# Input loads of later groups behind the weights, constant products in TensorE's planned pauses, and a last group that ends in two pairs

## The chip, the cores and the metric

The kernel runs on one core of one Trainium2 chip. The metric is the device time of one execution in microseconds (us). One core holds five engines with a queue each: TensorE (PE), VectorE (DVE), ScalarE (ACT), GpSimd (POOL) and SyncE (SP), which here issues nearly all transfers.

## The reference

There are 128 graphs of 128 nodes with 256 features each (`x`: 128 x 128 x 256) and an integer adjacency `adj` per graph. Four layers follow each other; each ends in a residual and a layer norm.

```python
A = (adj != 0)                               # layer 0: a gated graph network, 3 steps
for i in range(3):
    m = h @ weight[i]
    h = gru_cell(A^T @ m, h, w_ih, w_hh, b_ih, b_hh)
x = layernorm(x + h)
for W, a1, a2 in three attention layers:     # layers 1 to 3
    Wh = x @ W.T
    e = leaky_relu((Wh @ a1)[:, None] + (Wh @ a2)[None, :], 0.2)
    e = where(adj == 0, -huge, e)
    x = layernorm(x + softmax(e) @ Wh)
```

## The kernel before, in words

The 128 graphs are worked off in 32 groups of `G` = 4 graphs (512 columns). A group goes through `gru` (three steps of layer 0) and `gat` (layers 1 to 3), each with 128 partitions for the nodes or for one half of the features.

**Head.** Group 0 also prepares the weights. `hidden_weights` loads `w_hh` (two loads), scales it and builds the seven block sums of `whs` (`block_sums`, L432 to L436). `input_weights` multiplies each step's `gnn_wT` block with `w_ih` on TensorE (L466), evicts it with a scaling (L469, by `scale`, L411 or L413) and builds `wcs`. `transposed` (L555) turns the first two groups' x on TensorE; later groups are turned by transposing transfers (`turned`, L517). x is also split into three bf16 parts (L699), so that the sums over neighbours (L724) run in bf16.

**GRU.** A step multiplies both halves of the state and of the neighbour sums with the weights by a Strassen scheme (`strassen`, products at L650 into one of five PSUM tiles tagged `gate`). Between products into the same tile, ScalarE copies a partial sum out (L744, L748, L751) and VectorE adds (L655). The gates' arithmetic is at L762 to L801; the last step turns the state back on TensorE (L828) and adds it to x (L831); `layernorm` follows (L572 to L583).

**Attention.** A layer takes score sums on VectorE (L858, into a tile tagged `f` for one side), spreads one side over the columns (L870 and L877, or L887 for the last four groups), adds the mask and takes the maximum (L893), then Prelu (L897), Exp (L914), a transpose (L934 in the last four groups), the product with x (L964, four 128 x 128 products for each of two banks) and with W (L975, two products of 256 columns per graph), and the residual (L981). `deviation` squares on ScalarE with a sum (L591) and makes the variance (L595, L602); `power` raises it to -0.5 on GpSimd (L564). The scaling of layers 1 and 2 is folded into the next layer; the last one scales on ScalarE (L988) and stores the group (L990).

**Order.** No engine's order is written out by hand. Every operation is recorded with `plan.op(engines, fn, reads, writes, prio, ..., start)`: the engines that may run it with an assumed time in ns, its buffers, a priority and an earliest time. `Plan.order` plays the kernel through with these times (in four passes, with due times worked back from the pass before) and picks an engine, a slot of the buffer's pool and a place for each; it keeps the pass with the shortest end. Then the operations are emitted in that order, and each engine's queue holds its own in it. Times exist in the plan alone; on the chip an instruction waits only for its data, its buffers and its queue.

```python
plan.op({"SP": 450}, lambda e: nc.sync.dma_start(T(xs), x_g), writes=[xs], prio=prio)
...
order = plan.order()
with tc.manual_schedule():
    make_identity(nc, ident)
    nc.gpsimd.load_library(library_config.all_libraries[10])
    for o in order:
        o.fn(o.engine)
```

There are two slots each for x (`xs`) and the raw adjacency (`am`), three for `f`, five `gate` and three `bank` tiles in PSUM. The last four groups (`TAIL`) have a priority of their own and run their attention layers after the last GRU.

Of the kernel before, what the change touches and what calls it, by code (L numbers as in the profile page):

```python
# [12 lines left out]
AF = mybir.ActivationFunctionType  # L13
ALU = mybir.AluOpType
AX = mybir.AxisListType

P = 128
D = 256
KC = D // P
G = 4  # L20
# [6 lines left out]
EPS = 1e-5  # L27
# [281 lines left out]
def adj_resnorm_kernel(  # L309
# [14 lines left out]
    nc = tc.nc  # L324
    B = x.shape[0]
    NG = B // G
# [13 lines left out]
    tags = {t: (n, floats.get(t, 512)) for t, n in pools.items()}  # L340
    U16, BF16 = mybir.dt.uint16, mybir.dt.bfloat16
    BOTH = ("DVE", "POOL")
    LATER = (0.25, 1.75, -0.5, 0.25, 0.25, -1.0)
    plan = Plan({t: n for t, (n, _) in tags.items()}, own)
    slots = {t: [(psum if t in ("gate", "bank") else work).tile([P, w], F32, name=f"{t}{i}")
                 for i in range(n)] for t, (n, w) in tags.items() if w}

    def T(b):
        if b.at is None:
            width = 1  # L350
            for s in b.shape:
                width *= s
            at = slots[b.tag][b.slot][:, 0:width]
            if len(b.shape) == 2:
                at = at.rearrange("p (a b) -> p a b", b=b.shape[-1])
            elif len(b.shape) == 3:
                at = at.rearrange("p (a b c) -> p a b c", b=b.shape[-2], c=b.shape[-1])
            b.at = at
        return b.at
# [7 lines left out]
        return b  # L367

    for t in slots["f"]:
        nc.vector.memset(t, 0.0)  # L370

    nobody = [cycle([consts.tile([P, D], BF16, name=f"nobody{i}{j}") for j in range(2)]) for i in range(2)]
# [13 lines left out]
    neghalf = consts.tile([P, G], F32, name="neghalf")  # L388
# [20 lines left out]
    def scale(e, dst, src, by):  # L409
        if e == "ACT":  # L410
            nc.scalar.mul(dst, src, by)  # L411
        else:
            nc.vector.tensor_scalar(dst, src, by, None, op0=ALU.mult)  # L413
# [144 lines left out]
            res.append(dst)  # L558
        return res

    def power(ve, prio):

        rstd = Buf("v", G)
        plan.op({"POOL": 980}, lambda e: nc.gpsimd.tensor_tensor(T(rstd), T(ve), neghalf, ALU.pow),  # L564
                reads=[ve], writes=[rstd], prio=prio, port=BOTH, holds=False)
        return rstd

    def layernorm(y, dst, prio):
# [15 lines left out]
                T(dst)[:, b, :], T(y)[:, b, :], AF.Identity, bias=T(shift)[:, b:b + 1], scale=T(rstd)[:, b:b + 1]),  # L584
                reads=[(y, b), shift, rstd], writes=[(dst, b)], prio=prio)

    def deviation(y, before, prio):

        ss, ve = Buf("v", G), Buf("v", G)
        for b in range(G):  # L590
            plan.op({"ACT": 400}, lambda e, b=b: nc.scalar.activation(  # L591
                next(nobody[0]), T(y)[:, b, :], AF.Square, accum_out=T(ss)[:, b:b + 1]),
                reads=[(y, b)], writes=[(ss, b)], prio=prio, lag=85)
        if before is None:
            plan.op({"DVE": 78}, lambda e: nc.vector.tensor_scalar(  # L595
                T(ve), T(ss), 1.0 / D, EPS, op0=ALU.mult, op1=ALU.add),
                reads=[(ss, b) for b in range(G)], writes=[ve], prio=prio, port=BOTH)
        else:
            eps = Buf("v", G)
            plan.op({"DVE": 78}, lambda e: nc.vector.tensor_scalar(T(eps), T(before), EPS, None, op0=ALU.mult),  # L600
                    reads=[before], writes=[eps], prio=prio, port=BOTH)
            plan.op({"DVE": 78}, lambda e: nc.vector.scalar_tensor_tensor(  # L602
                T(ve), T(ss), 1.0 / D, T(eps), op0=ALU.mult, op1=ALU.add),
                reads=[(ss, b) for b in range(G)] + [eps], writes=[ve], prio=prio, port=BOTH)
        return ve

    def sums(ms, prio, banks=None, t=None):
# [24 lines left out]
    def strassen(gates, kept, prio):  # L632
# [40 lines left out]
        product(bx, N22, False)  # L673
        return o0, o1, bx

    def gru(g, stage):

        xs, ints = Buf("xs", G, D), Buf("am", G, P)
        prio = stage(g, 0)
        turn = Buf("gru")  # L680
        x_g = x[g * G:(g + 1) * G].rearrange("b n d -> n b d")
        plan.op({"SP": 450}, lambda e: nc.sync.dma_start(T(xs), x_g), writes=[xs], prio=prio)
        plan.op({"SP": 60}, lambda e: nc.sync.dma_start(T(ints).bitcast(I32), adj[g * G:(g + 1) * G].rearrange("b s t -> s b t")),
                writes=[ints], prio=prio)
        if g == 0:
            input_weights(0, (prio[0], -2))
            hidden_weights((prio[0], -2))
# [4 lines left out]
                reads=[ints], writes=[am, turn], prio=prio, port=BOTH)  # L692
# [20 lines left out]
        for i in range(STEPS):  # L713
            prio = stage(g, i)
# [129 lines left out]
    def gat(g, xc, far, stage):  # L844
# [5 lines left out]
        for l in range(3):  # L850
# [118 lines left out]
            for b0 in range(0, G, 2):  # L969
# [9 lines left out]
                for b in (b0, b0 + 1):  # L979
# [2 lines left out]
                                T(y)[:, b, :], T(b_)[:, (b - b0) * D:(b - b0 + 1) * D], T(rden)[:, b:b + 1],  # L982
                                T(xc)[:, b, :], op0=ALU.mult, op1=ALU.add),
                            reads=[b_, rden, (xc, b)], writes=[(y, b)], prio=prio)
            xc, ve = y, deviation(y, ve, prio)
            rstd = power(ve, prio)
        for b in range(G):
            plan.op({"ACT": 400}, lambda e, b=b: nc.scalar.mul(T(xc)[:, b, :], T(xc)[:, b, :], T(rstd)[:, b:b + 1]),  # L988
                    reads=[(xc, b), rstd], writes=[(xc, b)], prio=prio)
        plan.op({"SP": 60}, lambda e: nc.sync.dma_start(out[g * G:(g + 1) * G].rearrange("b n d -> n b d"), T(xc)),  # L990
                reads=[(xc, b) for b in range(G)], prio=prio)

    def stage(g, n):

# [4 lines left out]
        gat(g, *gru(g, stage), stage)  # L999

    order = plan.order()
    with tc.manual_schedule():
        make_identity(nc, ident)

        nc.gpsimd.load_library(library_config.all_libraries[10])
        for o in order:
            o.fn(o.engine)


# [40 lines left out]
```

## Time and profile before

| what | us |
|---|---|
| median of three runs (lowest, highest) | 2496.47 (2496.38, 2497.94) |
| the profiled execution: its own time | 2499.03 |
| its span, from the first to the last instruction | 2497.3 |
| TensorE, VectorE, ScalarE, GpSimd busy | 2459.4, 2192.5, 1950.0, 889.2 |
| gate products (L650) on the chain that ended last | 56% of the span |

The profile is of one execution. Its line numbers are those of the kernel before; in the changed kernel the same operations stand 2 to 21 lines further down up to the attention's end (L466 becomes L468, L555 L557, L564 L569, L591 L595, L650 L666, L724 L745, L744 L765, L828 L849, L887 L908, L934 L955, L964 L985, L975 L996, L981 L1002). A float32 product on TensorE appears as two records, so L964's eight products of a layer are x16. In a timeline a row gives start, length, engine, line, operation, tiles and count; in brackets stands how long the engine was idle before and what ended that.

### The profile page before, as it was taken

The page shows a single profiled execution, that of the slowest core. Times are in us where ns is not written, and L with a number is a line of the kernel's source. Part 1 is how long each engine was busy: PE and PEld are TensorE (multiplying, and loading weights), DVE is VectorE, ACT ScalarE, POOL GpSimd, SP SyncE. Part 2 cuts the span into 40 slices and gives each one's busy share as a digit, 9 for nine tenths or more (in the row PEclk, how much of TensorE's full clock was granted, in tenths as well). Part 3 has the DMA queues.
Part 4 walks back from the last instruction along what each step waited for, and adds up shares of the span by engine and source line. Part 5 has one row for each costly group of instructions (what it writes and reads, how often), then busy time and mean ns, then how long its engine had stood idle before and what let it go on. Part 6 is the DMA issues. An engine that isn't in the chain of part 4 may idle for free.

```text
span 2497.3 us, 42937 instructions
## 1 busy us (share of the span) xinstructions
PE 2459.4 (98%) x13716; PEld 2173.9 (87%) x13716; DVE 2192.5 (88%) x6443; ACT 1950.0 (78%) x4869; POOL 889.2 (36%) x1097
## 2 busy tenths in 40 slices
PE   8999999999999999999999999999999999999988
PEld 6888888888888888888888888888888888888877
DVE  6788899998998988989898989988989989877797
ACT  5667878888788887887977788887888877766578
POOL 3433335434334343345343344343343322212001
PEclk9999999999999999999999999999999999999989
DMA  5323323323423323333323333334333333010101
GB/s 140 64 42 65 81 65 76 73 57 75 82 64 77 72 54 75 81 65 76 75 54 77 81 64 72 61 72 77 76 69 69 73 63 68 22 39 18 39 1 35
DMA packets 456611, 161.41 MB, mean 65 GB/s; under 512 B 389184, under 2 KB 454720, under 8 KB 456384
## 3 DMA queue, kind: packets, MB, share of 16 engines
q1 hardware_dynamic: 455952, 158.65, 29.7%
q8 instruction: 108, 1.77, 0.3%
q14 instruction: 119, 0.97, 0.1%
q10 hardware_dynamic: 432, 0.01, 0.0%
HBM read 45.89 MB, written 16.78 MB: 25 GB/s over the span
## 4 chain that ended last, share of the span: by engine, by line
PE 77%; ACT 11%; DVE 8%; DMA 2%; issue 2%; POOL 0%; POOLq 0%; SPq 0%; ACTq 0%; DVEq 0%
PE gate L650 56%; PE bank L975 11%; PE bank L964 6%; PE bank L724 3%; ACT k L405 2%; ACT k L914 2%; DVE nobody L858 1%; DVE k L655 1%; ACT k L583 1%; ACT k L762 1%; DMA k<-k 1%; DVE k L981 1%; PE bank L728 1%; PE bank L466 1%; DMA xs<-in_x_dram 1%
## 5 line engine op out<-in xcount | busy, mean ns | idle before, releaser
L650 PE MATMUL gate<-k,whs 128*128 128x256 f32 x4032 | 1204.9, 380 | 9.7 <-ACT k L744 7.5
L650 PE MATMUL gate<-k,wcs 128*128 128x256 f32 x4032 | 1199.2, 379 | 0.0
L650 PEld LDWEIGHTS gate<-k,wcs 128*128 128x128 f32 x4032 | 766.0, 190 | 104.3 <-DVE k L407 0.2
L650 PEld LDWEIGHTS gate<-k,whs 128*128 128x128 f32 x4032 | 748.3, 190 | 120.9 <-issue 13.1
L655 DVE TENSOR_TENSOR k<-gate,k 128x512 f32<-128x512 f32 x576 | 391.6, 685 | 182.6 <-PE gate L650 121.3
L975 PE MATMUL bank<-gwT,k 128*128 128x256 f32 x1536 | 353.4, 382 | 0.6 <-DVE k L407 0.4
L564 POOL TENSOR_TENSOR v<-v,neghalf 128x4 f32<-128x4 f32 x128 | 154.2, 1204 | 526.3 <-DVE v L602 184.1
L858 DVE SCALAR_TENSOR_TENSOR nobody<-k,wa 128x256 bf16<-128x256 f32 x768 | 322.2, 463 | 4.4 <-ACT k L583 4.2
L975 PEld LDWEIGHTS bank<-gwT,k 128*128 128x128 f32 x1536 | 287.0, 190 | 38.8 <-DVE k L407 1.7
L762 ACT ACTIVATE k<-k,brz 128x512 f32<-128x512 f32 (+1 forms) x384 | 226.4, 620 | 76.8 <-DVE k L655 75.9
L405 ACT COPY k<-k 128x512 bf16<-128x512 bf16 (+1 forms) x308 | 223.5, 742 | 60.3 <-DVE k L801 42.9
L619 POOL TENSOR_TENSOR k<-k,k 128x256 f32<-128x256 f32 x257 | 207.2, 825 | 174.3 <-DVE k L801 127.7
L537 POOL TENSOR_TENSOR k<-k 128x512 f32<-128x512 f32 (+1 forms) x162 | 176.3, 1088 | 145.2 <-DVE k L801 66.2
L699 POOL TENSOR_TENSOR k<-xs 128x512 f32<-128x512 f32 x52 | 56.3, 1102 | 478.7 <-DMA xs<-in_x_dram 365.8
L591 ACT ACTIVATE nobody<-k 128x256 bf16<-128x256 f32 x384 | 156.2, 408 | 78.2 <-DVE k L981 78.1
L744 ACT COPY k<-gate 128x512 f32<-128x512 f32 x288 | 168.3, 585 | 61.9 <-PE gate L650 58.5
L877 POOL PARTITION_BROADCAST k<-k x336 | 154.1, 559 | 162.0 <-ACT k L405 85.9
L964 PEld LDWEIGHTS bank<-k,k 128*128 128x128 f32 x1536 | 187.3, 193 | 5.7 <-ACT k L405 0.8
L964 PE MATMUL bank<-k,k 128*128 128x128 f32 x1536 | 189.8, 277 | 0.9 <-ACT k L943 0.5
L511 ACT COPY k<-k 128x1024 uint16<-128x1024 uint16 x142 | 165.4, 1166 | 31.7 <-DMA k<-k 29.8
L405 ACT COPY k<-bank 128x512 f32<-128x512 f32 (+1 forms) x259 | 135.6, 530 | 64.2 <-PE bank L964 20.1
L897 ACT ACTIVATE k<-k,v 128x128 f32<-128x128 f32 x384 | 136.3, 399 | 59.9 <-DVE v L893 59.7
(117 smaller groups left out, 3580.5 us busy)
## 6 DMA issues: line engine op xcount, KB each, us to landing
xs<-in_x_dram SPq DMA_DIRECT2D x32, 512.0 KB, 4.0
k<-in_x_dram SPq DMA_DIRECT2D x32, 512.0 KB, 4.6
out_dram<-k SPq DMA_DIRECT2D x32, 512.0 KB, 3.4
am<-in_adj_dram SPq DMA_DIRECT2D x32, 256.0 KB, 2.9
k<-k SPq DMA_TRANSPOSE x366, 3.1
k<-in_gnn_wT_dram SPq DMA_DIRECT2D x3, 256.0 KB, 4.8
k<-in_w_ihT_dram SPq DMA_DIRECT2D x2, 384.0 KB, 6.3
k<-in_w_hhT_dram SPq DMA_DIRECT2D x2, 384.0 KB, 6.7
```

Source lines behind the costliest of these rows:

```text
L405: nc.scalar.copy(dst, src)
L511: nc.scalar.copy(flat().bitcast(U16).rearrange("p (q h) -> p q h", h=2), T(rows).bitcast(U16).rearrange("p (h q) -> p q h", h=2))
L537: nc.vector if e == "DVE" else nc.gpsimd).tensor_tensor(out(), T(whole), top(), ALU.subtract),
L591: plan.op({"ACT": 400}, lambda e, b=b: nc.scalar.activation(next(nobody[0]), T(y)[:, b, :], AF.Square, accum_out=T(ss)[:, b:b + 1]), reads ...
L619: nc.vector if e == "DVE" else nc.gpsimd).tensor_tensor(T(t)[:, j, :], a(), b(), ALU.subtract),
L650: nc.tensor.matmul(T(dst)[:, j * H:(j + 1) * H], T(w)[:, m, gt, :], moving(m, ms)[1](), start=first and n == 0, stop=n == len(todo) - 1, s ...
L655: plan.op({"DVE": 602}, lambda e: nc.vector.tensor_add(T(o)[:, :, j * H:(j + 1) * H], T(b_).rearrange("p (g n) -> p g n", g=2), T(part).re ...
L744: plan.op({"ACT": 475}, lambda e: nc.scalar.copy(T(dst), T(src)), reads=[src], writes=[(dst, 0), (dst, 1)], prio=prio)
L762: nc.scalar.activation(T(o)[:, gt, n0:n1], src(), AF.Tanh, bias=brz[:, gt * KC + c:gt * KC + c + 1], scale=0.5)
L858: plan.op({"DVE": 345}, lambda e, b=b, h=h, l=l, side=side, xc=xc: nc.vector.scalar_tensor_tensor(next(nobody[1]), T(xc)[:, b, :], 1.0, T( ...
L964: nc.tensor.matmul(T(b_)[:, b * P:(b + 1) * P], T(xc)[:, b, c * P:(c + 1) * P], T(pT)[:, b, :], start=True, stop=True)
L975: nc.tensor.matmul(T(b_)[:, (b - b0) * D:(b - b0 + 1) * D], T(aT[k])[:, b * P:(b + 1) * P], T(gwT)[:, l, k, :], start=(k == 0), stop=(k == ...
```

## The change

The points of the change, and what they come to in the built program:

1. The loads of x and adjacency of all groups but the first get an earliest time of 9000 ns in the plan.
2. `idle_product` multiplies the first `f` tile with itself (128 x 128 by 128 columns, float32) into the first 128 columns of a `gate` tile that nobody uses at that time; the result is never read. Eight stand at the head of TensorE's queue. After planning, each pause of TensorE that the plan shows as longer than `FILL` = 400 ns gets one for each 223 ns above it, put in front of the operation that the pause ends at. So that the operands aren't zero, the `f` tiles start with ones.
3. In the built program there are 16 of them in the head (8 in front of the first transposes, 8 behind them), none in the middle, and 57 from the end of the last GRU on: 16, 7, 13, 2 and 3 until the first L996, two single ones, and 4, 6 and 4 in the last two layers' ends.
4. In the last layer of the last group the variance, the power, the scaling and the store are done for graphs 0 and 1 and for graphs 2 and 3 by themselves, and squares and scalings may go to VectorE too.

The core of the diff:

```diff
+    FILL = 400
+    WEIGHTS = 9000
...
     for t in slots["f"]:
-        nc.vector.memset(t, 0.0)
+        nc.vector.memset(t, 1.0)
...
-    def power(ve, prio):
+    WHOLE = ((0, G),)
+
+    def power(ve, prio, parts=WHOLE):
         rstd = Buf("v", G)
-        plan.op({"POOL": 980}, lambda e: nc.gpsimd.tensor_tensor(T(rstd), T(ve), neghalf, ALU.pow),
-                reads=[ve], writes=[rstd], prio=prio, port=BOTH, holds=False)
+        for b0, b1 in parts:
+            plan.op({"POOL": 980}, lambda e, b0=b0, b1=b1: nc.gpsimd.tensor_tensor(
+                T(rstd)[:, b0:b1], T(ve)[:, b0:b1], neghalf[:, b0:b1], ALU.pow),
+                reads=[(ve, b0)], writes=[(rstd, b0)], prio=prio, port=BOTH, holds=False)
...
+    def square(e, y, b, ss):
+        if e == "ACT":
+            nc.scalar.activation(next(nobody[0]), T(y)[:, b, :], AF.Square, accum_out=T(ss)[:, b:b + 1])
+        else:
+            nc.vector.scalar_tensor_tensor(next(nobody[1]), T(y)[:, b, :], 1.0, T(y)[:, b, :], op0=ALU.mult, op1=ALU.mult,
+                                           accum_out=T(ss)[:, b:b + 1])
...
+    def idle_product(dst, n):
+        for _ in range(n):
+            nc.tensor.matmul(dst[:, 0:P], slots["f"][0], slots["f"][0], start=True, stop=True)
...
-        plan.op({"SP": 450}, lambda e: nc.sync.dma_start(T(xs), x_g), writes=[xs], prio=prio)
+        plan.op({"SP": 450}, lambda e: nc.sync.dma_start(T(xs), x_g), writes=[xs], prio=prio, start=WEIGHTS * (g > 0))
         plan.op({"SP": 60}, lambda e: nc.sync.dma_start(T(ints).bitcast(I32), adj[g * G:(g + 1) * G].rearrange("b s t -> s b t")),
-                writes=[ints], prio=prio)
+                writes=[ints], prio=prio, start=WEIGHTS * (g > 0))
...
-            xc, ve = y, deviation(y, ve, prio)
-            rstd = power(ve, prio)
+            parts = ((0, 2), (2, G)) if g == NG - 1 and l == 2 else WHOLE
+            xc, ve = y, deviation(y, ve, prio, parts)
+            rstd = power(ve, prio, parts)
+        for b0, b1 in parts:
+            for b in range(b0, b1):
+                plan.op({"ACT": 400} if parts == WHOLE else {"ACT": 400, "DVE": 340}, lambda e, b=b: scale(
+                    e, T(xc)[:, b, :], T(xc)[:, b, :], T(rstd)[:, b:b + 1]),
+                    reads=[(xc, b), (rstd, b0)], writes=[(xc, b)], prio=prio, port=("DVE", "POOL") if parts != WHOLE else ())
+            plan.op({"SP": 60}, lambda e, b0=b0, b1=b1: nc.sync.dma_start(
+                out[g * G + b0:g * G + b1].rearrange("b n d -> n b d"), T(xc)[:, b0:b1]),
+                reads=[(xc, b) for b in range(b0, b1)], prio=prio)
...
     order = plan.order()
+    filled, ends, since, until = {}, None, {}, {}
+    for n, o in enumerate(order):
+        for b in o.bufs:
+            if b.tag == "gate":
+                since.setdefault(b.slot, n)
+                until[b.slot] = n
+    for n, o in enumerate(order):
+        if o.engine == "PE":
+            gap = o.start - ends if ends is not None else 0
+            ends = o.start + o.engines["PE"]
+            unused = [slot for slot in until if until[slot] < n or since[slot] > n]
+            if gap > FILL and unused:
+                filled[o] = unused[0], int((gap - FILL) // 223) + 1
     with tc.manual_schedule():
         make_identity(nc, ident)
+        idle_product(slots["gate"][0], 8)
         nc.gpsimd.load_library(library_config.all_libraries[10])
         for o in order:
+            if o in filled:
+                idle_product(slots["gate"][filled[o][0]], filled[o][1])
             o.fn(o.engine)
```

More of the change, by code (lines that the diff above doesn't have):

```diff
@@ L585, in layernorm, with deviation @@
                 reads=[(y, b), shift, rstd], writes=[(dst, b)], prio=prio)
-    def deviation(y, before, prio):
+    def square(e, y, b, ss):
[4 more added lines that the diff above has]
+                                           accum_out=T(ss)[:, b:b + 1])
+    def deviation(y, before, prio, parts=WHOLE):
         ss, ve = Buf("v", G), Buf("v", G)
+        engines = {"ACT": 400} if parts == WHOLE else {"ACT": 400, "DVE": 345}
         for b in range(G):
[L591 to L598, printed above, removed]
+            plan.op(engines, lambda e, b=b: square(e, y, b, ss),
+                    reads=[(y, b)], writes=[(ss, b)], prio=prio, lag=85, port=("DVE", "POOL") if parts != WHOLE else ())
+        if before is not None:
             eps = Buf("v", G)
@@ L601, in deviation @@
                     reads=[before], writes=[eps], prio=prio, port=BOTH)
-            plan.op({"DVE": 78}, lambda e: nc.vector.scalar_tensor_tensor(
-                T(ve), T(ss), 1.0 / D, T(eps), op0=ALU.mult, op1=ALU.add),
-                reads=[(ss, b) for b in range(G)] + [eps], writes=[ve], prio=prio, port=BOTH)
+        for b0, b1 in parts:
+            sums_of = [(ss, b) for b in range(b0, b1)]
+            if before is None:
+                plan.op({"DVE": 78}, lambda e, b0=b0, b1=b1: nc.vector.tensor_scalar(
+                    T(ve)[:, b0:b1], T(ss)[:, b0:b1], 1.0 / D, EPS, op0=ALU.mult, op1=ALU.add),
+                    reads=sums_of, writes=[(ve, b0)], prio=prio, port=BOTH)
+            else:
+                plan.op({"DVE": 78}, lambda e, b0=b0, b1=b1: nc.vector.scalar_tensor_tensor(
+                    T(ve)[:, b0:b1], T(ss)[:, b0:b1], 1.0 / D, T(eps)[:, b0:b1], op0=ALU.mult, op1=ALU.add),
+                    reads=sums_of + [eps], writes=[(ve, b0)], prio=prio, port=BOTH)
         return ve
@@ L984, in gat @@
                             reads=[b_, rden, (xc, b)], writes=[(y, b)], prio=prio)
-            xc, ve = y, deviation(y, ve, prio)
-            rstd = power(ve, prio)
[L987 to L991, printed above, removed]
+            parts = ((0, 2), (2, G)) if g == NG - 1 and l == 2 else WHOLE
+            xc, ve = y, deviation(y, ve, prio, parts)
+            rstd = power(ve, prio, parts)
+        for b0, b1 in parts:
+            for b in range(b0, b1):
[5 more added lines that the diff above has]
+                reads=[(xc, b) for b in range(b0, b1)], prio=prio)
     def stage(g, n):
```

## Prediction

> **What bounds the kernel now.** I read the page first, then the waits of TensorE, the chain of waits of the first 80 us, the timeline of both ends, and the table by stage round the last pause. On the page:
>
> ```profile
> PE 2459.4 (98%) x13716; PEld 2173.9 (87%) x13716; DVE 2192.5 (88%) x6443; ACT 1950.0 (78%) x4869; POOL 889.2 (36%) x1097
> ```
>
> TensorE is busy for 2459.4 of 2497.3 us. Only the 38 us in which it isn't, and work that it does at half rate, can be won. The waits of TensorE (us in total, times, longest) say where most of them lie:
>
> ```profile
> PE bank L555 <- DMA xs<-in_x_dram: 10.9, 2, 5.9
> PE gate L650 <- ACT k L744: 7.5, 27, 0.5
> PE bank L828 <- DVE k L801: 4.9, 2, 3.6
> ```
>
> The head loses 10.9 us to x, the end of the last GRU 4.9, and the long middle 7.5 in 27 small pieces. After the last matmul come 8.5 us more of evictions, norm and store. The chain of the head (start, length, what):
>
> ```profile
> 5.25 7.56 DMA xs<-in_x_dram
> 12.85 1.11 PE bank L555 x4
> 13.97 7.57 PE bank L466 x16
> ...
> 23.32 7.77 PE gate L650 x36
> 31.09 5.16 PE bank L466 x16
> ```
>
> The second group's x holds the chain from 5.25 to 12.81, and the weight products (L466) queue behind its transposes. The same 16 records take 7.57 us here and 5.16 at 31.09: the head runs at half rate at first. Round the last pause the granted clock stands in the table by stage (busy us by engine, then clock, DMA share, GB/s):
>
> ```profile
> 2395.00:2400.00 5.00, 3.38 (x19) 2.48 (x17) 5.00 (x14) 3.57 (x8) 0.00 (x0) 1.00 0.00 0
> 2400.00:2405.00 5.00, 1.60 (x7) 1.21 (x8) 4.82 (x18) 2.23 (x6) 0.00 (x0) 0.62 0.01 3
> 2405.00:2410.00 5.00, 3.16 (x12) 1.75 (x11) 5.00 (x32) 4.47 (x20) 1.18 (x1) 0.50 0.00 0
> 2410.00:2415.00 5.00, 5.00 (x22) 4.91 (x23) 3.65 (x19) 3.22 (x9) 0.00 (x0) 0.52 0.00 0
> 2415.00:2420.00 5.00, 5.00 (x33) 4.61 (x33) 4.98 (x23) 4.04 (x19) 0.00 (x0) 1.00 0.02 3
> ```
>
> The pause halves the clock (0.50) until about 2415. But VectorE (the third busy time) is full in those stages, except for 1.35 us at 2410 to 2415.
>
> **The head.** Moving x and mask changes little on the queue: in the built program's order the first seven transfers are as before, and one weight block goes ahead of the second x. What moves is TensorE's order: those transposes (L555, now L557) stand behind the weight products and the sums of the first group. So the weight products no longer wait for 12.85, but for their weights: the two w_ih blocks are issued at 2.31 to 3.2 and land 6.3 us after their issue (median of the two), so at about 9.1. Eight constant products stand ahead of the first transposes and eight behind them. They have the shape of L964, whose eight products (16 records) take 3.57 us from the first start to the next group's at half clock, 1.78 at full: 0.446 and 0.223 us each. The first eight (3.6 us) lie in the 5 us in which TensorE waited for x; the other eight (1.8 to 3.6) start at about 6.8 and end at 8.6 to 10.4, so cost at most 1.3.
>
> What is late next is VectorE. There are three banks for four weight products; the fourth reuses the first's, which VectorE empties in its own order behind the scaling of w_hh:
>
> ```profile
> 11.34 0.63 ACT L411 ACTIVATE k<-k 128x512 f32<-128x512 f32 x1 [0.39 <-DMA k<-in_w_hhT_dram]
> 14.61 1.45 DVE L413 TENSOR_SCALAR k<-k 128x256 f32<-128x256 f32 x2
> 15.98 1.39 DVE L434 TENSOR_TENSOR whs<-k 128x384 f32<-128x384 f32 x1
> 17.42 0.69 DVE L413 TENSOR_SCALAR k<-bank 128x512 f32<-128x512 f32 x1
> ```
>
> w_hh is there at 11.34, and VectorE took 3.4 us from 14.61 to the eviction's end near 18.0; before, its queue was stuck at the eviction of the second x until 14.01. Now it starts at 11.35, the bank is free at about 14.8, the fourth product (two of 0.43) ends at 15.7. In the trace the last weight product ends at 21.54 and the first gate product starts at 23.32, 1.78 later: now 17.5, or 5.8 us earlier. Four transposes of the second x (0.44) now follow later, leaving 5.4. A new wait follows: ScalarE's eviction of the second sums bank stands ahead of the first gate eviction and waits for four VectorE additions; I take off 0.5: 4.9. Lower bound: only VectorE's earlier start counts, 14.61 - 11.35 = 3.3, less 0.44 = 2.8. Upper: VectorE holds nothing, 9.1 + 5.16 + 1.78 = 16.0, so 7.3 - 0.44 = 6.8. I take 4.9 since the row of the same evictions is nearest.
>
> The clock rule: the trace shows 0.50 still granted at 2410 to 2415, though TensorE had been full from 2409.95. [...]
>
> A second row speaks against the change: L434 took 1.39 us at 15.98 under GpSimd's run and 0.55 at 19.47. [...] I took the slow row for these steps, so nothing is added.
>
> **The middle.** Neither the number of matmuls nor the distance from a gate product to the next use of its bank differs between the two orders (the same 26 close pairs), and no constant product stands there. The 7.5 us of waits stay, give or take 1.5.
>
> **The last GRU's pause.** Constant products of 16, 7, 13, 2 and 3 stand there in the built order. The pauses before were 3.57, 1.38, 1.44 and 0.40; 16 at 0.223 are 3.57, so they fit. They hold the clock up. The cold rows lose at most 3.9 us: L828 twice 0.5, L934 and L887 0.9 together, L964 1.8, L934 and L975 0.7 less what VectorE hides. VectorE's spare time there is 1.35 + 0.18 = 1.5, and the last three products read f's first tile, which VectorE writes for the next stage: they wait for its third score sum, and its fourth waits for them. By rows: L964's evictions end at 2413.1 and that sum at 2413.4, three products (0.67) bring the L975 stage to 2414.1 where it started at 2414.38. With full clock for its first half I take 0.5 won; bounds -0.6 (no clock gain, the 0.67 in full) and 3.9. After that VectorE is full to 2470, which keeps the gain but adds none; two single products there cost 0.1 together (0 to 0.45).
>
> **The end.** The last rows:
>
> ```profile
> 2485.44 3.29 PE L975 MATMUL bank<-gwT,k 128*128 128x256 f32 x14 [0.20 <-DVE k L407]
> 2487.04 0.88 DVE L981 SCALAR_TENSOR_TENSOR k<-bank,v,k 128x256 f32<-128x256 f32 x2 [1.66 <-PE bank L975]
> 2488.83 0.88 DVE L981 SCALAR_TENSOR_TENSOR k<-bank,v,k 128x256 f32<-128x256 f32 x2 [0.92 <-PE bank L975]
> 2490.59 1.01 POOL L564 TENSOR_TENSOR v<-v,neghalf 128x4 f32<-128x4 f32 x1 [5.30 <-DVE v L602]
> 2491.64 1.71 ACT L988 ACTIVATE k<-k,v 128x256 f32<-128x256 f32 x4 [1.32 <-POOL v L564]
> ```
>
> From 2487.04 the store is issued 6.3 us later. In pairs, with a square and a scaling of each pair on VectorE, the first power (1.01) lies under the second pair's matmul; then: second evictions to 2.67, square to 3.1, a scaling 0.35, variance 0.15, power to 4.7, scalings on two engines to 5.2, issue at 5.25: 1.06 earlier. The last store has half the bytes; 512 KB took 0.31 to 0.33 of 5 us of all DMA engines, 1.6, so half saves 0.8. Together 1.9 (0.7 to 2.6, as far as the small powers and the fixed part of a store are unknown). Against it stand constant products of 4, 6 and 4. The real pauses are shorter than the planned ones, since the first half product ran ahead of the second eviction (2477.42) and L964 started at ScalarE's first scaled tile (2482.50). Behind four products (0.89) that half comes late: 0.36. Six (1.34) put L964 at 2483.2, 0.7 late, of which ScalarE's pace hides 0.2: 0.5. The last four: 0.4. Together 1.25 (0 to 14 x 0.223 = 3.1).
>
> **The sum:** 4.9 + 0.5 - 0.1 + 1.9 - 1.25 = 5.95 us. Against the profiled span 2497.3 that is 2491.3, against its own time of 2499.03, 2493.1; the median of the runs is 2496.47, so I predict 2490.5. 0.2% (5 us) is about what a measurement of this kernel can tell from no change.
>
> **Rivals.** *VectorE is the head* (20%): the 6.0 us in which VectorE waited at 14.01 are for the change, GpSimd's port and the sums' order against; the gain is then the lower 2.8, and with 0.5 - 0.1 + 1.9 - 1.25 makes 3.9: 2492.6, or 2494.5 if the tail gives nothing and the new head wait doubles. *The constant products are paid in full* (7%): the 57 in the tail take 12.7 us; if f's tile ties TensorE and VectorE together at each group, so that the real pauses (6.8 us) aren't covered, then 4.9 + 1.9 - 12.7 = -5.9: 2502.4. It turns slower where over 6.8 us of the 12.7 stay visible. Only three groups need that wait in the built order, which is against it. [...]
>
> **The chances.** Forecast 73%, with a range of its own of 2487.0 to 2492.5 (4 to 9.5 us; the top from the head's 6.8 and the pause's larger gain). About 7 of the 73 lie at 4 to 5 us and count as no change, as do the 20 of the first rival and 1 of the second. So faster 0.66, same 0.28, slower 0.06. The range takes in the first rival: 2487.0 to 2494.5.
>
> **What would show it.** L468 starts at 9 to 10.4, the first L666 near 17.5, with VectorE's L415 on w_hh at 11.4. The clock stays 1.00 at 2395 to 2415 of the old count, yet the first L996 comes only 0.3 earlier. The middle's waits on L765 stay near 7.5. The last store is issued 5.2 us after the first eviction of the last L996. I am wrong if L666 starts after 20, if waits of TensorE in the middle grow by over 3 us, or if constant products are followed by work that was ready before them.

## The result, and the profile after

The changed kernel is slower: 2517.42 us median (2514.16 to 2517.54) against 2497.94 for the kernel before in the same session, a ratio of 1.0077 (95% interval 1.0062 to 1.0091). Its profiled execution spans 2514.2 us, 16.9 more than before. Lines of the changed kernel have moved by 2 to 21: L666 is the gate product (L650), L765 ScalarE's copy of a partial sum (L744), L513 and L409 the copies of transposed data (L511, L407), L996 the last product (L975).

The page's line of busy times, and then the waits of TensorE (us in total, times, longest):

```profile
PE 2479.5 (99%) x13862; PEld 2184.3 (87%) x13862; DVE 2200.4 (88%) x6444; ACT 1948.4 (77%) x4866; POOL 896.8 (36%) x1101
```

```profile
PE gate L666 <- ACT k L765: 11.9, 22, 1.9
PE gate L666 <- ACT k L772: 4.3, 7, 0.8
PE gate L666 <- DVE k L635: 2.4, 3, 0.9
PE gate L666 <- DVE k L671: 2.0, 5, 0.6
PE bank L468 <- DVE k L415: 1.5, 1, 1.5
```

The head's wait for x (10.9 before) is down to 0.2, and the cold pause's wait for L801 (4.9) is gone. The gate products wait 20.6 us in all. Before, they waited 9.4, since two small sources come on top of the 7.5 for L744:

```profile
PE gate L650 <- ACT k L751: 1.7, 3, 0.7
PE gate L650 <- DVE k L655: 0.2, 1, 0.2
```

These two (now L772 and L671) have grown, L635 is new, and the longest single waits are longer.

Where the time went is read by counting the records of gate products (two for each product, numbered from 0), of which both kernels have 8064 in the same order. Time from the span's start (us) at which a given one starts:

| | before | changed | difference |
|---|---|---|---|
| first | 23.16 | 17.23 | -5.9 |
| number 168 | 78.32 | 77.19 | -1.1 |
| number 504 | 156.80 | 155.67 | -1.1 |
| number 7560 | 2257.7 | 2276.4 | +18.7 |
| last | 2398.1 | 2416.8 | +18.7 |
| end of the span | 2497.3 | 2514.2 | +16.9 |

The head wins 5.9 and gives 4.8 back by 78 us; the end wins 1.8; between products 504 and 7560, called the middle from here, 19.9 us are lost (2100.9 before, 2120.8 after). Nothing was edited there, and each engine's instructions stand in the same order; only slots and banks differ. About half of the loss shows as idle time of TensorE (10.0 us in the middle before, 20.4 after); the other half counts as busy time of the same products, at a granted clock of 1.00 in both, because their records last a little longer or overlap less. What stretches them was not followed up.

The waits on transposing transfers (`k<-k`) name what comes late. First before, then changed; VectorE's copies and ScalarE's:

```profile
DVE k L407 <- DMA k<-k: 0.4, 1, 0.4
ACT k L511 <- DMA k<-k: 29.8, 37, 3.5
```

```profile
DVE k L409 <- DMA k<-k: 6.9, 10, 1.4
ACT k L513 <- DMA k<-k: 41.4, 50, 3.5
```

The queues issue these transfers in the same order, and their median from issue to landing is 3.1 us in both pages. So a minority lands late, and a median doesn't show it.

### The profile page after: what moved, and what is told of

It is laid out like the page before. It is cut to its first block, busy times and chain, and to the rows that moved or that the text cites. A ratio compares the mean times of both kernels' runs of the same rounds, so it can differ in the third digit from the quotient of the medians.

```text
span 2514.2 us, 43236 instructions
## 1 busy us (share of the span) xinstructions
PE 2479.5 (99%) x13862; PEld 2184.3 (87%) x13862; DVE 2200.4 (88%) x6444; ACT 1948.4 (77%) x4866; POOL 896.8 (36%) x1101
## 4 chain that ended last, share of the span: by engine, by line
PE 70%; DVE 13%; ACT 11%; DMA 4%; issue 2%; POOL 1%; SPq 0%; POOLq 0%; DVEq 0%; ACTq 0%
PE gate L666 51%; PE bank L996 10%; PE bank L985 5%; DMA k<-k 3%; PE bank L745 3%; DVE nobody L879 2%; ACT k L407 2%; DVE k L671 2%; ACT k L935 1%; DVE k L1002 1%; ACT k L589 1%; ACT k L513 1%; ACT k L783 1%; DVE k L409 1%; PE bank L749 1%
## 5 line engine op out<-in xcount | busy, mean ns | idle before, releaser
L666 PE MATMUL gate<-k,whs 128*128 128x256 f32 x4032 | 1207.5, 381 | 19.3 <-ACT k L765 11.9
L666 PE MATMUL gate<-k,wcs 128*128 128x256 f32 x4032 | 1199.8, 379 | 2.7 <-DVE k L635 2.4
L666 PEld LDWEIGHTS gate<-k,whs 128*128 128x128 f32 x4032 | 746.3, 190 | 138.3 <-issue 13.7
L666 PEld LDWEIGHTS gate<-k,wcs 128*128 128x128 f32 x4032 | 765.5, 190 | 109.1 <-DVE k L635 5.1
L671 DVE TENSOR_TENSOR k<-gate,k 128x512 f32<-128x512 f32 x576 | 391.3, 684 | 179.3 <-PE gate L666 115.7
L996 PE MATMUL bank<-gwT,k 128*128 128x256 f32 x1536 | 353.1, 382 | 1.2 <-DVE k L1002 0.7
L996 PEld LDWEIGHTS bank<-gwT,k 128*128 128x128 f32 x1536 | 286.6, 190 | 40.4 <-DVE k L1002 2.8
L407 ACT COPY k<-k 128x512 bf16<-128x512 bf16 (+1 forms) x310 | 224.9, 742 | 63.3 <-DVE k L822 45.6
L635 POOL TENSOR_TENSOR k<-k,k 128x256 f32<-128x256 f32 x259 | 211.9, 837 | 165.2 <-DVE k L822 124.6
L539 POOL TENSOR_TENSOR k<-k 128x512 bf16<-128x512 f32 (+1 forms) x163 | 177.2, 1087 | 144.2 <-ACT nobody L595 65.8
L765 ACT COPY k<-gate 128x512 f32<-128x512 f32 x288 | 168.3, 585 | 60.7 <-PE gate L666 58.3
L513 ACT COPY k<-k 128x1024 uint16<-128x1024 uint16 x142 | 165.3, 1165 | 41.4 <-DMA k<-k 41.4
L407 ACT COPY k<-bank 128x512 f32<-128x512 f32 (+1 forms) x260 | 136.0, 530 | 65.0 <-PE bank L985 18.3
```

Of the source, the lines that this page charges most:

```text
L407: nc.scalar.copy(dst, src)
L513: nc.scalar.copy(flat().bitcast(U16).rearrange("p (q h) -> p q h", h=2), T(rows).bitcast(U16).rearrange("p (h q) -> p q h", h=2))
L539: nc.vector if e == "DVE" else nc.gpsimd).tensor_tensor(out(), T(whole), top(), ALU.subtract),
L635: nc.vector if e == "DVE" else nc.gpsimd).tensor_tensor(T(t)[:, j, :], a(), b(), ALU.subtract),
L666: nc.tensor.matmul(T(dst)[:, j * H:(j + 1) * H], T(w)[:, m, gt, :], moving(m, ms)[1](), start=first and n == 0, stop=n == len(todo) - 1, s ...
L671: plan.op({"DVE": 602}, lambda e: nc.vector.tensor_add(T(o)[:, :, j * H:(j + 1) * H], T(b_).rearrange("p (g n) -> p g n", g=2), T(part).re ...
```

## The experiments

In each table row the ratio is to the kernel before, run on the same chip, with its 95% interval; the middle is that of the one profiled execution. "Ahead" counts the constant products that stand in the head, ahead of the middle. The planned pauses put 7 there with the old order of x and mask, 8 with the new one, and 57 in the tail; the explicit call adds 8. That the pauses reach into the head was overlooked when the first expectations were written: where they say "tail alone", 7 stand in the head too.

| run | ahead | us | ratio | middle, us |
|---|---|---|---|---|
| before | 0 | | | 2100.9 |
| changed | 16 | 2517.42 | 1.0077 (1.0062, 1.0091) | 2120.8 |
| e1 no order | 15 | 2520.13 | 1.0092 (1.0077, 1.0107) | 2124.4 |
| e2 order only | 0 | 2492.23 | 0.9983 (0.9973, 0.9992) | 2097.7 |
| e3 products only | 15 | 2521.52 | 1.0096 (1.0081, 1.0111) | 2123.5 |
| e4 no products | 0 | 2490.15 | 0.9972 (0.9961, 0.9984) | 2096.2 |
| e5 head, zeros | 8 | 2492.25 | 0.9989 (0.9979, 0.9998) | 2095.6 |
| e6 planned pauses, zeros | 7 | 2496.75 | 1.0004 (0.9994, 1.0013) | 2099.2 |
| e7 ones only | 0 | 2495.70 | 1.0001 (0.9992, 1.0011) | 2098.5 |
| e8 changed, zeros | 16 | 2516.12 | 1.0077 (1.0061, 1.0094) | 2123.6 |
| e9 head, ones | 8 | 2493.22 | 0.9992 (0.9983, 1.0001) | 2097.4 |
| e10 changed, 24 | 32 | 2516.25 | 1.0085 (1.0070, 1.0100) | 2122.1 |
| e11 order, pairs, head | 8 | 2491.10 | 0.9983 (0.9974, 0.9992) | 2098.0 |
| e12 72 at the end | 0 | 2498.24 | 1.0009 (0.9999, 1.0018) | 2104.7 |
| e13 changed, 64 at the end | 16 | 2514.27 | 1.0069 (1.0052, 1.0085) | 2121.1 |
| e14 changed, 24 at the end | 16 | 2513.35 | 1.0066 (1.0051, 1.0081) | 2118.6 |
| e15 changed, no explicit call | 8 | 2495.05 | 0.9991 (0.9982, 1.0001) | 2101.9 |
| e16 before, 16 tiny | 16 | 2518.60 | 1.0090 (1.0075, 1.0105) | 2120.6 |
| e17 before, 64 tiny | 64 | 2499.49 | 1.0016 (1.0006, 1.0025) | 2100.6 |
| e18 changed, 48 tiny | 64 | 2492.26 | 0.9986 (0.9976, 0.9996) | 2099.8 |

**Which part loses.** My first theory was that the new order of x and mask moves the middle's buffers to other slots (it does) and so delays transfers; the rivals were the constant products, and chance. e1 is the changed kernel with

```diff
-    WEIGHTS = 9000
+    WEIGHTS = 0
```

> x and mask of the later groups keep their old place, the constant products and the pairs at the end stay. Only the late start of x and mask moves the buffers and banks of the middle; with the old place they are those of the kernel before. Theory one (the order's buffers): the middle's 19.9 us are gone, the end's 1.8 us stay won, the head wins little: 2494 to 2496 against 2497. Theory two (constant products, by a clock held in the head or by ones instead of zeros): the middle stays 20 us longer, 2514 to 2517. Theory three (the loss was chance of one execution or one loading): no difference outside 0.2%.

e2 keeps the new order and takes the rest away (no explicit call, no products in the pauses, f set to zeros, no pairs):

```diff
-        idle_product(slots["gate"][0], 8)
...
-            if gap > FILL and unused:
+            if False and gap > FILL and unused:
...
-            parts = ((0, 2), (2, G)) if g == NG - 1 and l == 2 else WHOLE
+            parts = WHOLE
```

> Only the late start of x and mask; no constant product, no pairs. Theory one: -5.9 in the head (some 1 to 3 us less without products that hold the clock), +4.8 at 20 to 57 us, +19.9 in the middle: about 2515 to 2519 against 2497. Theory two: 2490 to 2493. Theory three: no loss.

e3 has `WEIGHTS = 0` and `parts = WHOLE`, so only the products; e4 only drops the products (the first two edits of e2, and zeros).

> Only the constant products (eight in the head, the ones in the planned pauses of the tail); buffers and order as before. Theory one: head and tail within 1.5 us of before, 2496 to 2498. Theory two: the middle 20 us longer, 2515 to 2518. By my forecast's step for the tail (0.5 won in the last GRU's pause, 0.1 and 1.25 lost): 0.85 us later, plus the head's clock, up to 3 us earlier.

> The late start of x and mask and the pairs at the end, without any constant product. Theory one: as the changed kernel within 3 us, 2514 to 2518. Theory two: 2488 to 2492. The difference from the run with the late start alone is what the pairs bring: 1.9 by my forecast.

The theory fell: e1 and e3 lose with the old slots and order, e2 and e4 win with the new ones. The products cost the 20 us; order and pairs together win 6.6 us (2496.78 to 2490.15).

**Which products, and by what.** e5 to e7 take the kernel before and add one thing: the explicit call over zeros, the planned pauses' products over zeros, and ones in f without a product.

> The kernel before with the eight constant products of the head alone, over zeros instead of ones. The products cost the middle some 20 us, though nothing in the middle differs but what lies before or after it. Theory four (the place in TensorE's instruction stream: eight products more ahead of the middle move the 16 KB blocks in which the instructions are fetched against the groups' work): all of the loss is here, 2515 to 2520 against 2497. Theory five (the ones that stay in f): 2494 to 2498.

> The kernel before with the constant products of the planned pauses in the tail alone, over zeros. They stand behind the middle in TensorE's stream. Theory four: no loss in the middle, what the tail itself gives: 2496 to 2498. A theory six (the length or place of the whole program in memory): 2515 to 2520.

> The kernel before with f set to ones instead of zeros and no constant product. The column that is used is written for each group; the other columns keep the ones and go through the transposes. Theory four: 2496 to 2498, as before. Theory five: 2515 to 2520.

None of the three loses, though theory four had all of the loss in e5 (2515 to 2520). So it looked as if two of them had to act together. e8 is the changed kernel with `memset(t, 0.0)`; e9 is e5 over ones; e10 has `idle_product(slots["gate"][0], 24)` in the changed kernel; e11 is e4 with the explicit call, over zeros.

> The changed kernel with f set to zeros: the same instructions, the constant products multiply zeros. Head alone, tail alone and ones alone each left the middle as it was; so the loss needs two of the three together. Theory four (place and length of TensorE's stream, head and tail together; what is multiplied is of no account): 2515 to 2520 against 2497. Theory seven (products over ones, as against zeros): 2487 to 2491.

> The kernel before with the eight products of the head over ones, none in the tail. Theory four: as with zeros, 2491 to 2495. Theory seven: 2513 to 2520.

> The changed kernel with 24 constant products at the head's start instead of 8: 32 more TensorE passes ahead of the middle, a quarter of the 128 or so between two fetches of its code, so that the fetches fall elsewhere in each group's work. Theory four: the loss of the middle changes by over 5 us, most likely down, 2495 to 2515, of which at most 3.6 us is what the 16 products (0.223 each) cost in the head. Theory seven: 2517 to 2522, as the changed kernel or up to 3.6 us more.

> The late start of x and mask, the pairs at the end and the eight products of the head over zeros, none in the tail. Theory four: the head's place alone did no harm with the old order; 2487 to 2491 if that holds with the new one. Theory seven: 2487 to 2491 too, as there are no ones. [...]

What is multiplied is of no account: e8 loses, e9 doesn't. e10 missed theory four's guess that the loss would shrink; it stayed.

e12 to e14 try the length of TensorE's stream alone, with products of one column by one column (tiny products, about 0.05 us each) behind the last matmul: 72 in the kernel before, 64 and 24 in the changed kernel. e15 is the changed kernel without the explicit call.

```diff
             o.fn(o.engine)
+        for _ in range(72):
+            nc.tensor.matmul(slots["gate"][0][0:1, 0:1], slots["f"][0][:, 0:1], slots["f"][0][:, 0:1], start=True, stop=True)
```

> The kernel before with 72 small constant products (one column by one column) behind its last matmul and none elsewhere: as many passes of TensorE in all as in the run with the products of head and tail, with nothing before, in or next to the middle changed. They lie under the last norm and store, or end the run up to 5 us later. Theory eight (the length of TensorE's stream decides how hard its code fetches hit the transposing transfers): the middle 20 us longer, 2515 to 2522. Theory nine (head and tail must both hold products at their places): middle as before, 2496 to 2502.

> The changed kernel with 64 small products behind its last matmul, some 16 KB more of code. Theory eight: another length can bring the lighter fetches back, 2487 to 2497 with the end up to 5 us later; or it stays at 2515 to 2522 if every longer stream is slow. Theory nine: 2515 to 2522.

> The changed kernel with 24 small products behind its last matmul. Theory eight: 2487 to 2492 or 2514 to 2518, not between; a second point of the length. Theory nine: 2514 to 2518.

> The changed kernel without the eight products of the head: late start of x and mask, pairs, and the 64 products of the planned pauses over ones. Theory eight, if this length is still on the fast side as it was with the old order: 2488 to 2492, and beside the run without any product (2490.2) it shows what the tail's products give; by my forecast 0.85 us worse. If this length is over the edge: 2515 to 2518.

The length is not it (e12, e13 and e14 keep their sides). e15 is on the fast side too, but at 2495.05 it misses its 2488 to 2492; its middle takes 5.7 us more than e4's, which is not explained. Counting where the products stand then left one rule: with 0, 7 or 8 ahead the middle takes 2095.6 to 2104.7 us, with 15, 16 or 32 it takes 2118.6 to 2124.4, some 20 us more.

**The code fetches.** One of the page's two instruction queues is read here as TensorE's code: q8 has 108 packets before, of 1.77 MB in all, 16 KB each, beside 13716 passes with a weight load each, and 109 in the changed kernel, which has 73 products (146 passes) more; with 64 more still, in e13, it has 110. The other queue (q14) has 119 in both pages. So one fetch comes every 127 passes on average, about 23 us. A constant product is two passes and two loads (13862 against 13716 passes for 73); by this count 64 of them fill one fetch, 16 a quarter. Products ahead of the middle would then move all later fetches against the groups' work, by a quarter of 23 us for 16, and not at all for 64. e16 and e17 put tiny products alone into the head of the kernel before, and e18 adds 48 to the 16 of the changed kernel:

```diff
+        for _ in range(16):
+            nc.tensor.matmul(slots["gate"][0][0:1, 0:1], slots["f"][0][:, 0:1], slots["f"][0][:, 0:1], start=True, stop=True)
         nc.gpsimd.load_library(library_config.all_libraries[10])
```

> The kernel before with 16 products of one column by one column at the head's start (0.05 us each, where TensorE waits for x) and nothing else. Every slow run so far had 15 or 16 products in the head or more (the planned pauses put 7 or 8 of them there too, so the run of the tail alone had 7 in the head), every fast one 8 or fewer. Theory four, now by the head's count alone: 16 products are 32 passes and 32 weight loads, a quarter of what lies between two fetches of 16 KB, and move the fetches onto the landing of the transposing transfers: 2512 to 2520. Against it (the products' own work, the tail, or an earlier head): 2494 to 2498.

> The kernel before with 64 such small products in the head. Theory four: 64 products are 128 passes and 128 weight loads, as much as lies between two fetches, so the fetches fall where they did: 2494 to 2500, fast although four times as many products stand there. If more products are simply worse: above 2515.

> The changed kernel whole, with 48 small products added to the 16 constant products of its head: 64 in all. Theory four: the loss of the middle goes, 2489 to 2497, some 20 us faster than the changed kernel by adding work to it. Against it: 2514 to 2520.

All three came out as the fetches' place says. The traces show the place itself: counted in passes of the kernel's own work, a fetch of the middle starts (median) 98 passes behind the last one of the kernel before in e16 and 61 in e10, where a shift by 32 and by 64 passes in blocks of 127 gives 95 and 63; in e17 it is 1.5. Sixteen tiny products, under 1 us of work beside a wait for x, cost 23 us; 64 leave the middle as it was (2100.6 against 2100.9), though e17 as a whole is 3.9 us above the kernel before, which is not explained; and 48 more bring the changed kernel from 1.0077 of the kernel before to 0.9986, some 23 us, by adding work to it. The waits follow. TensorE's in e18 (before: 7.5), then VectorE's and ScalarE's for transposed data in e16 and in e17:

```profile
PE gate L666 <- ACT k L765: 7.6, 24, 0.6
```

```profile
DVE k L407 <- DMA k<-k: 6.8, 10, 1.3
ACT k L511 <- DMA k<-k: 39.5, 49, 4.2
```

```profile
DVE k L407 <- DMA k<-k: 0.8, 2, 0.4
ACT k L511 <- DMA k<-k: 32.3, 39, 3.5
```

One transfer shows how. The transposing transfer that is issued at 211.20 in the kernel before and at 212.29 in e16 has the same bytes. The transfer view of the 6 us from 0.4 us ahead of each issue (40 slices of 0.15 us), before:

```profile
DMA  0000000000299999999200000000000000000000
GB/s 0 0 0 0 0 0 0 0 0 0 53 212 225 217 215 203 205 205 180 35 0 0 0 0 0 0 0 0 0 0 0 0 0 0 0 0 0 0 0 0
...
k<-k SPq DMA_TRANSPOSE x1, 3.0
```

And in e16:

```profile
DMA  0000000000399999999900000002000000000000
GB/s 0 0 0 0 0 0 0 0 0 0 65 212 225 213 208 316 201 186 133 19 0 0 7 9 10 9 10 35 0 0 0 0 0 0 0 0 0 0 0 0
...
q8 instruction: 1, 0.02, 1.0%
...
k<-k SPq DMA_TRANSPOSE x1, 4.5
```

Nearly all packets pass in the same 1.5 us. But a code fetch (q8; its packet runs from 214.28 to 215.25) falls among them, and a remainder follows from the slice at 215.2 on, at 7 to 10 GB/s: just when the fetch has ended. The full rate before, 203 to 225 GB/s over 16 engines, is 13 to 14 each, so I read the remainder as what one engine moves that had the fetch ahead of its share. That the two share an engine is read from these rates; the trace doesn't name a packet's engine. The landing comes behind the last of these packets in both: before at 214.24, with packets up to 213.8, and in e16 at about 216.8, with packets up to 216.1, so 4.5 us after issue in place of 3.0. VectorE's copy of that data, before and in e16:

```profile
215.13 0.74 DVE L407 COPY k<-k 128x1024 uint16<-128x1024 uint16 x1
215.76 0.68 DVE L798 SCALAR_TENSOR_TENSOR k<-k,k 128x512 f32<-128x512 f32 x1
```

```profile
216.77 0.75 DVE L407 COPY k<-k 128x1024 uint16<-128x1024 uint16 x1 [0.47 <-DMA k<-k]
217.41 0.68 DVE L798 SCALAR_TENSOR_TENSOR k<-k,k 128x512 f32<-128x512 f32 x1
```

The copy had come 0.9 us behind the landing (215.13 against 214.24); now, with a landing 1.4 us later after its issue, it waits, and everything behind it on VectorE is late by another 0.5. The next transposing transfer is issued 1.64 us late where this one was 1.09 late, and at 243.1 (old count) TensorE loses 0.68 us. The same step recurs at 695.1, 1147.0 and 1599.9: some 452 us, six groups, apart.

Over the middle (150 to 2260 us) I counted, of the 189 or 190 transfers of this line (L517, or L519), those in which a fetch starts 0.75 to 2.75 us after issue, and their mean time to landing. Without such a fetch it is 3.11 to 3.15 us in every run. No expectation had named this window ahead of the runs.

| run | ahead | transfers hit | their mean, us |
|---|---|---|---|
| before, e17, e18 | 0, 64, 64 | 7, 6, 5 | 3.90, 3.89, 3.68 |
| e4, e5 | 0, 8 | 4, 10 | 3.76, 3.59 |
| e16, changed | 16, 16 | 21, 25 | 4.36, 4.19 |
| e3, e10 | 15, 32 | 20, 18 | 4.10, 4.17 |

Over all runs, those that lose the 20 us have 18 to 25 transfers hit (means 4.10 to 4.36 us), the others 4 to 13 (3.42 to 3.97). On the other line of transposing transfers (L541, or L543) hits don't tell the runs apart: 11 to 23 where the time is lost, 14 to 24 where it isn't.

A rival is that TensorE itself stands still while its code is fetched. Lining up the products of two traces one by one speaks against it. Of the 19.7 us by which the middle of e16 falls behind the kernel before, 0.6 arises within 3 us of a fetch's start (15% of the time), but 20.6 within 30 us of the landing of a hit transfer (27% of the time); the rest makes up for 0.9. For the changed kernel against e4 it is 0.7 and 21.1 of 24.6 us (35% of the time).

## Why the prediction was wrong

**The step that failed** is the middle: "Neither the number of matmuls nor the distance from a gate product to the next use of its bank differs between the two orders (the same 26 close pairs), and no constant product stands there. The 7.5 us of waits stay, give or take 1.5." The premises held, the conclusion didn't: waits of gate products went from 9.4 to 20.6 us (the step had left out 1.9 of the 9.4), and the middle cost 19.9. The prediction's own sign of being wrong, waits in the middle that grow by over 3 us, came true. What I left out is that 16 products ahead are 64 more instructions, which move the fetches behind them. The page showed the queue (q8, 108 packets) and I passed it over at 0.3% of the DMA engines' time. With 64 products ahead, the middle takes what this step said (2099.8 in e18).

**The head.** Its landmarks held: the weight products start at 8.41 (said: 9 to 10.4, so 0.6 early), VectorE's scaling of w_hh at 10.96 (11.4), the fourth weight product waits for VectorE's bank until 14.40 (14.8), the first gate product starts at 17.23 (17.5). In the timeline of the changed kernel, TensorE's rows, then VectorE's:

```profile
8.41 4.46 PE L468 MATMUL bank<-k,k 128*128 128x512 f32 x12
14.40 1.13 PE L468 MATMUL bank<-k,k 128*128 128x256 f32 x4 [1.52 <-DVE k L415]
...
17.23 0.60 PE L666 MATMUL gate<-k,whs 128*128 128x256 f32 x2
```

```profile
10.96 1.47 DVE L415 TENSOR_SCALAR k<-k 128x512 f32<-128x512 f32 x2 [3.11 <-DMA k<-in_w_hhT_dram]
...
14.74 1.39 DVE L436 TENSOR_TENSOR wcs<-k 128x384 f32<-128x384 f32 x1
...
19.20 1.39 DVE L434 TENSOR_TENSOR wcs<-k,k 128x384 f32<-128x384 f32 x1
...
21.51 1.39 DVE L435 TENSOR_TENSOR wcs<-wcs,k 128x384 f32<-128x384 f32 x1
```

Mis-sized was what follows. I took the slow row (1.39 us) for the sums of `whs` and wrote that "nothing is added". The sums of `wcs`, 0.55 us each before at 19.47 to 24.05, now ran at up to 1.39, and the gate products behind them waited 3.0 us up to 78 us (before: none), where I had put 0.5 for a new wait. GpSimd is busy there for 5.00 us of 15 to 20 and for 4.80 of 20 to 25; that its run is the cause was argued from the row before, not tried. Of 4.9 us forecast, 1.1 were left at product 504; e8, with the same instructions, kept 3.9, and e2, without products, 3.6. The range between the first two is not explained. The clock did open early: the 16 passes of the first eight products start at 1.04 and take 3.78 us, the trace's first record of a granted clock is 1.00 from 6.46 on, behind most of the transposes too, and the second eight take 1.95 us from 6.63. In e8 it is granted from 4.22 on, before the first eight have ended. So with the same instructions the moment was 6.46 in one execution and 4.22 in another; why is not shown.

**The last GRU's pause and the end.** The clock was held, as forecast. The table by stage of the changed kernel (busy us by engine, then clock, DMA share, GB/s) has the clock at 1.00 through the pause that had stood at 0.50:

```profile
2419.00:2424.00 5.00, 5.00 (x43) 4.62 (x42) 5.00 (x21) 2.52 (x7) 0.00 (x0) 1.00 0.01 3
2424.00:2429.00 5.00, 4.48 (x40) 4.27 (x39) 5.00 (x34) 4.50 (x21) 1.18 (x1) 1.00 0.00 0
2429.00:2434.00 5.00, 3.96 (x30) 3.56 (x29) 3.74 (x18) 4.87 (x17) 0.00 (x0) 1.00 0.00 0
```

VectorE is full in the first two of these stages. Counted from the last gate product, the first L996 comes 0.25 us earlier with the products than without in e4 (15.88 against 16.13; forecast 0.3), and the group near 74 us 0.32 (73.59 against 73.91; forecast 0.5). But over all runs the first L996 stands at 15.88 or 15.89 with these products and anywhere from 15.31 to 16.31 without, so the 0.5 of the sum is not shown. (Its upper bound of 3.9 is a slip as well: the terms listed there add up to 4.4.) The last three places then lost 1.07 (forecast 1.25): the first eviction of the last L996 stands at 89.57 against 88.82 in e4. The pairs brought 1.93 (98.55 us from the last gate product to the end in e2, 96.62 in e4; forecast 1.9), of it 0.8 in the last store, which lands in 2.1 us with half the bytes, where the whole one took 2.9 (these two views are of e2 and e4):

```profile
out_dram<-k SPq DMA_DIRECT2D x1, 512.0 KB, 2.9
```

```profile
out_dram<-k SPq DMA_DIRECT2D x2, 256.0 KB, 2.1
```

So the products of the tail cost 0.75 us net against e4 (97.36 against 96.62) and 1.0 against e11 (96.33), which also has pairs and no products there. The sum has 0.85 (0.5 - 0.1 - 1.25): near, with a gain in it that isn't shown.

**The rivals.** "The constant products are paid in full" had the right sign for a wrong reason: the 57 products of the tail cost 0.75 to 1.0 us, not 12.7. "VectorE is the head" describes what the head gave back, if not its size; no run shows the port of GpSimd that it names, only that L434 before took 1.39 us at 15.98 while GpSimd ran and 0.55 at 19.47 when it didn't. That the clock would not be held fell: it stands at 1.00 where it had stood at 0.50. None of them was the fetches, so the 6% for slower stood for a mechanism that didn't act.

**What would be kept.** The late x and mask (with pairs: e4, 2490.15, the fastest run). Beside it, constant products gain nothing measurable even where their count leaves the fetches alone: e18 is at 2492.26, and e4, without any, ran in another session at 2490.15.

**Open.** Of the counts ahead only 0, 7, 8, 15, 16, 32 and 64 were tried, and no way to move the transfers rather than the fetches. Which place is good or bad is known only by trying. e10's fetches stand another quarter further on, hit fewer transfers of this line (18) and lose as much, but not in the same way: nearly half of its loss is two events. A transfer that is hit lands 4.80 us after its issue at 293.08, another 4.56 us after 753.48; TensorE then waits 4.09 us (until 309.21) and 3.89 (until 769.42) for L765, and the granted clock stands at 0.50 for 6.8 and 3.4 us. The two cost 6.5 and 5.7 us against e4. In no other run did the clock fall in the middle.

## What to carry to other kernels

Work added to a long unrolled stream is also code: before calling an insertion free, count its instructions against the code fetches (here 16 KB, every 127 passes of TensorE) and look at which transfers with a reader close behind them land while a fetch passes. When a kernel loses time far from any edit, with the same order and the same medians, compare the k-th instruction of both traces for where the loss begins and recurs, then test by shifting the stream with instructions that cost next to nothing (here about 0.05 us each), a quarter of a block and a whole one. Compare variants at the same count of instructions ahead, or a difference of 1% may be the fetches' place (here 2518.60 us with 16 tiny products ahead, 2499.49 with 64).

## What the runs showed of the hardware

A fetch of 16 KB, read as TensorE's code, is one packet of about 1 us (median 0.99 of the 108 before), and all fetches together take 0.3% of the DMA engines' time. Yet a transposing transfer of 256 KB (L517) that a fetch meets at 0.75 to 2.75 us after issue lands later: after 3.4 to 4.4 us in the means of the runs, against 3.1. The runs with 18 to 25 such meetings in 2100 us lose about 20 us of TensorE's time beside those with 4 to 13. Counted in passes of the kernel's own work, the fetches of the middle stood (median) 98 behind the last one of the kernel before with 16 products ahead (e16), 61 with 32 (e10) and 1.5 with 64 (e17), and one of the losses of e16 comes four times, six groups apart. In these runs the loss went with the count of instructions ahead and not with their work: with 16 products of about 0.05 us the middle took 2120.6 us, with 16 of 0.24 to 0.47 it took 2120.8, and with 64 of 0.05 it took 2100.6, against 2100.9 with none. In e10 two waits of TensorE of 4.09 and 3.89 us in the middle went with a clock of 0.50 for 6.8 and 3.4 us; in the changed kernel the waits of gate products were at most 1.9 us each, and the clock stayed at 1.00 through the middle.
